# Conv pieces of a deformable layer in other slots of a hand-written schedule

## The chip, the core and the metric

The kernel runs on one core of one Trainium2 chip. The metric is the device time of one execution in microseconds, here the median of several runs. Engine names: PE is TensorE, DVE is VectorE, ACT is ScalarE, POOL is GpSimd, SP is SyncE, whose queue issues most of the DMAs.

## What is computed

A net of four layers over x[8, 384, 32, 32] in fp32: a state-space layer, a deformable layer, a second state-space layer with an MLP, and a displacement layer. Each adds its result to its input after a group norm. The change is in the deformable layer only:

```python
def deform_block(x, ow, ob, dw, pw, pb, K):
    offsets = conv2d(x, ow, ob, K // 2)              # 2*K*K maps: dy, dx of every tap
    out = deform_depthwise(x, offsets, dw, K, K // 2)  # bilinear samples, weighted, summed over taps
    return conv2d(out, pw, pb, 0)                    # 1x1

c3, c5, c7 = jnp.split(x, 3, axis=1)                 # 128 channels each
out = jnp.concatenate([deform_block(c3, ..., 3), deform_block(c5, ..., 5), deform_block(c7, ..., 7)], axis=1)
return out * se_weight(out, fc1_w, fc2_w)
```

with x the group norm of the layer's input (32 groups, so mean and variance over 12 channels and all 1024 pixels).

## The kernel before

The layer is `deform_fast`. It handles the 8 samples one after the other, and of each sample three blocks: 3x3, 5x5, 7x7. The taps of a block are gathered in fours ("quads"; the last one has a single tap), and each quad is done in two halves. One half of one quad is a **unit**: 6 units in the 3x3 block, 14 in the 5x5 block, 26 in the 7x7 block, 46 in a sample, 368 in all.

A unit needs four steps. SP loads the sampling positions (`positions`, L1417). ACT turns them into bilinear "hat" functions in x and y (`unit_hats`, L1433 to L1451; the x hats are made once for both halves, with the first). DVE weighs the transposed input (`fxk`, L1469) and multiplies x and y hats into products (`fsm`, L1486, five buffers). PE multiplies the two and adds into five PSUM banks (`wacc`, L1516).

All of this stands in a hand-written order. Time is cut into **slots**, one for each unit. In slot u the program emits the position loads of unit u+4, the products of PE for unit u, the DVE work of unit u+1 and the hats of unit u+2; the loop is at the end of `deform_fast`. Everything else is put into a slot by `put(slot, place, fn, ...)` in `block_steps`, where place says the engine (`pe`, `dve`, `act`) and whether it comes ahead of the slot's unit work (`pe0`, `dve0`, `act0`) or behind it (`pe1`, `dve1`, `act1`). For PE, DVE and ACT this order is kept as it is written (`manual_schedule`). The engines are not tied to one another but for their data, so a slot has no fixed length.

The slots concerned, by name:

- `first[b, g]` is the slot of the first unit of block g (0, 1, 2 for 3x3, 5x5, 7x7) of sample b; `s0` is that of the block at hand. The 3x3 and 5x5 blocks together have 20 slots, the 7x7 block 26.
- For g = 0 the base t is `s0 - 26`, which is the start of the 7x7 block of the sample in front. From there on, in that block: the load of the new sample (`load`, L1096), group-norm statistics (`stats`, L1102, DVE), group means by a matmul (`mean`, L140), deviations (`dev`), their squares on ACT (`square`, L167), a second matmul (`mean2`, L150), variance, 1/std on ACT with two table loads (`rstd`, L181 and L182), then the normalisation of each third of the channels (`norm`, L1126, DVE), and last the 3x3 conv in one piece of 36 matmuls (`conv`, L1195, PE) and the step that takes its result (`offsets`, L1206 to L1217: add, write to DRAM, maxima and minima).
- For g = 1 the 5x5 conv has 50 matmuls in six pieces, one a slot, also in the 7x7 block in front.
- For g = 2 the 7x7 conv is done as a fast convolution (`fir`, L1157) in three parts with 21, 28 and 28 matmuls of up to 512 columns. `fir_sum` (L1143, DVE) makes the sums of even and odd columns that part 0 reads. After each part its result is taken from PSUM: `fir_take` on ACT for part 0 (L1166), on DVE for parts 1 and 2 (L1171). `fir_end` (L1178 to L1182) adds the grid, finds maxima and minima, and writes the positions.
- All three convs use one PSUM bank (`ps_off`, tag "conv", one buffer), so each conv or part starts after the one ahead of it has been read.

At the start of each block, `sums_act` closes the old accumulation with five matmuls of zeros (L1254), ACT and DVE add its banks up (L1256 to L1262), and `begin` opens the new one with five more (L1397). Around there the transposed input is made too: `rows_pe` (L1223) and `cells_pe` (L1243) on PE, copied out by ACT (L1230, L1248). `point` (L1268) is the 1x1 conv, `squeeze` (L1281 to L1283) the sums and maxima of the squeeze gate.

Of the kernel before, what the change touches and what calls it, by code (L numbers as in the profile page):

```python
# [17 lines left out]
G = C // P  # L18
# [73 lines left out]
class Net:  # L92
# [984 lines left out]
    def block_steps(self, b, g, first, put, weights, src, dst):  # L1077
        nc, K = self.nc, KS[g]
        K2, pad = K * K, K // 2
# [246 lines left out]
        if g == 0:  # L1326
            t = s0 - 2 * len(QUADS[KS[-1]])
            put(t + 1, "act0", load)
            for i in range(G):
                put(t + 2 + i, "dve1", stats, i)  # L1330
            put(t + 6, "pe0", mean)
            put(t + 6, "dve1", dev)
            put(t + 7, "act1", square)
            put(t + 8, "pe0", mean2)
            put(t + 8, "dve1", var)
            put(t + 9, "act1", rstd)
            for i in range(G):
                put(t + 10 + i, "dve1", norm, i)
            put(t + 13, "pe1", conv, 0, 0, K2)
            put(t + 14, "dve0", offsets, 0)  # L1340
        elif g == 1:
            t = first[b, 0] - 12
            for i in range(6):
                put(t + i, "pe1", conv, 0, K2 * i // 6, K2 * (i + 1) // 6)
            put(t + 6, "dve0", offsets, 0)
        else:
            t = first[b, 0]
            put(t - 1, "dve1", fir_sum)
            k = 0
            for part, pieces in enumerate((4, 5, 5)):  # L1350
                nw = K * len(FIR[part])
                for i in range(pieces):
                    where = "pe0" if t + k in (first[b, 0], first[b, 1]) else "pe1"
                    put(t + k, where, fir, part, nw * i // pieces, nw * (i + 1) // pieces)
                    k += 1
                put(t + k, "dve0" if part else "act0", fir_take, part)
            put(t + k, "dve0", fir_end)
# [490 lines left out]
```

## Time and profile before

| | us |
|---|---|
| median of 3 runs | 9464.09 |
| lowest, highest | 9463.35, 9469.98 |
| profiled execution | 9470.15 |
| its span, first to last instruction | 9468.3 |
| mean granted TensorE clock | 0.947 |
| PE busy in the span | 8498.2 |
| DVE busy | 8092.7 |
| ACT busy | 6476.0 |

The profile is one execution taken by the hardware profiler. A timeline row has the start in us, the duration, the engine, the line of the kernel, the operation, output and input by the program's names, the shape and the number of instructions merged into the row; in brackets the idle time of the engine ahead of it, and what ended that. One fp32 matmul leaves two records. A row of the windows table has the length of the window and, for each engine, the busy time in it with the number of instructions, then the granted TensorE clock, the busy share of the DMA engines, and GB/s.

The deformable layer lies between about 3031 and 5862 us. The zeroing at L1397, which opens a block, begins at 3117.78 for the first 3x3 block and at 3457.07, 3802.93, 4150.08, 4495.93 for the next samples' 3x3 blocks; the 7x7 blocks of the first three samples open at 3273.64, 3618.10 and 3963.95. Other rows of use:

| row | number |
|---|---|
| 7x7 conv matmuls (L1157), records | 1232 |
| 3x3 and 5x5 conv matmuls (L1195), records | 1376 |
| products on PE (L1516), records | 10624 |
| PE waiting for DVE's products ahead of L1516, in all | 240.5 us, 278 times |
| DVE waiting for PE ahead of the products of L1486, in all | 315.6 us, 320 times |

### The profile page before, as it was taken

Reading aid. Unit: us, or ns where it says so; the run is one execution under the profiler, and the core shown is the slowest. Engines: PE = TensorE matmul, PEld = TensorE weight load, DVE = VectorE, ACT = ScalarE, POOL = GpSimd, SP = SyncE. Lnnn points to the kernel's source line nnn. Section 1 sums busy time; section 2 is a strip of 40 time slices with the busy share of each in tenths; the row PEclk is TensorE's granted clock in tenths of the full one; section 3 lists DMA queues with packets and bytes.
Section 4 is the critical chain, followed back from the end, with each engine's and each line's share of the span. In section 5 each row is a group of like instructions: output and inputs, shape, how many; then the busy total and the mean of one; then the engine's idle time right before and its main releaser. Section 6 shows DMA issues by size and latency. Waiting matters only on the chain. (4 is left out here: it accounts for less than half of the span.)

```text
span 9468.3 us, 87246 instructions
## 1 busy us (share of the span) xinstructions
PE 8498.2 (90%) x27916; PEld 4527.1 (48%) x27916; DVE 8092.7 (85%) x8857; ACT 6476.0 (68%) x10147; POOL 5825.0 (62%) x3825
## 2 busy tenths in 40 slices
PE   7888888889887999999999997699999999999987
PEld 3333333333333677777777776244343443434333
DVE  7989999999997678778778877899999999999973
ACT  6666666666664678778778777667777777777750
POOL 7989989898897000000000000899999999999974
PEclk8999999999998999999999998799999999999998
DMA  2111211121121333333333333233232433323436
GB/s 94 66 56 46 85 56 49 52 83 56 50 79 40 80 77 89 92 80 88 89 83 87 90 80 87 93 99 96 90 95 88 126 107 96 92 91 90 123 99 127
DMA packets 566064, 791.97 MB, mean 84 GB/s; under 512 B 244243, under 2 KB 397235, under 8 KB 542041
## 3 DMA queue, kind: packets, MB, share of 16 engines
q1 hardware_dynamic: 503492, 775.85, 28.2%
q10 hardware_dynamic: 62100, 10.44, 0.7%
q8 instruction: 223, 3.65, 0.2%
q14 instruction: 249, 2.03, 0.1%
HBM read 716.49 MB, written 69.66 MB: 83 GB/s over the span
## 5 line engine op out<-in xcount | busy, mean ns | idle before, releaser
L443 POOL TENSOR_TENSOR db<-du,bc 128x1024 f32<-128x1024 f32 x1536 | 3607.0, 2354 | 356.3 <-DVE hs L453 184.7
L453 DVE TENSOR_TENSOR_SCAN da<-da,db 128x1024 f32<-128x1024 f32 x1248 | 2857.4, 2290 | 220.5 <-ACT da L438 170.0
L484 PE MATMUL y<-hs,ident 128*128 128x512 f32 x5184 | 2602.9, 639 | 382.2 <-DVE hs L467 229.8
L438 ACT ACTIVATE da<-dt,na 128x512 f32<-128x512 f32 x3072 | 2119.4, 691 | 917.0 <-DVE hs L467 653.8
L411 POOL TENSOR_TENSOR dt<-dt,sp_e 128x512 f32<-128x512 f32 x192 | 243.9, 1270 | 2929.1 <-DVE sp_e L403 2929.1
L484 PEld LDWEIGHTS y<-hs,ident 128*128 128x128 f32 x5184 | 1020.4, 203 | 1860.6 <-issue 1115.9
L1516 PE MATMUL wacc<-fsm,fxk 128*128 128x221 f32 (+34 forms) x10624 | 1667.7, 316 | 91.5 <-DVE fsm L1486 88.8
L1516 PEld LDWEIGHTS wacc<-fsm,fxk 128*128 128x128 f32 x10624 | 1580.6, 196 | 228.4 <-DVE fsm L1486 151.7
L467 DVE TENSOR_TENSOR hs<-da,bc 128x1024 f32<-128x1024 f32 x1248 | 1528.5, 1225 | 91.7 <-DVE da L453 2.3
L1486 DVE TENSOR_TENSOR fsm<-fhy,fhx 128x170 f32<-128x170 f32 (+42 forms) x3216 | 1171.5, 431 | 342.5 <-PE wacc L1516 315.6
L1446 ACT ACTIVATE fhy<-fpyx,cell 128x416 f32<-128x416 f32 (+9 forms) x1280 | 645.6, 576 | 386.8 <-DVE fsm L1486 386.8
L1469 DVE TENSOR_TENSOR fxk<-fxt,fwk 128x1024 f32<-128x1024 f32 (+1 forms) x688 | 788.2, 1182 | 10.8 <-ACT fxt L1248 10.8
L464 POOL TENSOR_TENSOR hs<-hs,bc 128x1024 f32<-128x1024 f32 x288 | 678.3, 2355 | 41.7 <-ACT st L459 41.6
L453 DVE TENSOR_TENSOR_SCAN hs<-da,db 128x1024 f32<-128x1024 f32 x288 | 656.8, 2280 | 49.0 <-POOL db L431 36.1
L471 POOL TENSOR_TENSOR hs<-hs 128x512 f32<-128x512 f32 x480 | 608.9, 1268 | 4.0 <-DVE hs L467 3.5
L567 PE MATMUL ps_m<-hid,wm 128*128 128x512 f32 x1152 | 536.8, 611 | 30.2 <-ACT hid L560 25.3
L545 PE MATMUL ps_h<-t,wm 128*128 128x512 f32 x1152 | 535.9, 603 | 16.5 <-DVE x L574 16.3
L1451 ACT ACTIVATE fhy<-fhy,cols 128x1344 f32<-128x1344 f32 (+10 forms) x368 | 530.8, 1442 | 12.0
L459 ACT COPY st<-da 128x2 f32<-128x2 f32 x624 | 97.8, 157 | 504.3 <-DVE hs L467 503.0
L1157 PE MATMUL ps_off<-fxn,fow 128*98 128x465 f32 (+10 forms) x896 | 386.6, 579 | 0.0
L1433 ACT ACTIVATE fhx<-fpyx,cell 128x544 f32<-128x544 f32 (+8 forms) x640 | 379.9, 666 | 0.0
L567 PEld LDWEIGHTS ps_m<-hid,wm 128*128 128x128 f32 x1152 | 221.6, 195 | 330.8 <-issue 262.4
(203 smaller groups left out, 9865.4 us busy)
## 6 DMA issues: line engine op xcount, KB each, us to landing
bc<-bcd SPq DMA_DIRECT2D x256, 1024.0 KB
fpyx<-fposd SPq DMA_DIRECT2D x640, 256.0 KB
wm<-in_w SPq DMA_DIRECT2D x96, 768.0 KB
x<-x SPq DMA_DIRECT2D x71, 768.0 KB
winr<-in_win SPq DMA_DIRECT2D x192, 192.0 KB
x<-in_x SPq DMA_DIRECT2D x40, 768.0 KB
fpyx<-fposd SPq DMA_DIRECT2D x24, 1024.0 KB
wm<-in_wout SPq DMA_DIRECT2D x48, 384.0 KB
```

The lines of the kernel that those rows point to most:

```text
L438: nc.scalar.activation(da[:, i, :], s["dt", j], AF.Exp, scale=na[:, j, n : n + 1])
L443: nc.gpsimd.tensor_tensor(db, du, s["bc"][m][:, 0], ALU.mult)
L453: nc.vector.tensor_tensor_scan(h1, da1, db1, 0.0, ALU.mult, ALU.add)
L464: nc.gpsimd.tensor_tensor(s["hs", m], s["hs", m], c, ALU.mult)
L467: nc.vector.tensor_tensor(hs, s["da", m], c, ALU.mult)
L471: nc.gpsimd.tensor_tensor(hs[:, 0, :], hs[:, 0, :], hs[:, 1, :], ALU.add)
L484: nc.tensor.matmul(s["y"], self.ident, s["hs", m][:, i, :], start=first and i == 0, stop=k == NU - 1 and i == n - 1,)
L567: nc.tensor.matmul(ps, s["w2"][:, f, o * P : (o + 1) * P], s["hid", q][:, f, :], start=(f == 0), stop=(f == 3))
L1446: nc.scalar.activation(hy[:, at : at + (yb - ya) * W], pyx[:, 0, ya * W : yb * W], AF.Abs, bias=bias)
L1469: nc.vector.tensor_tensor(t[:, :n], x, wk[:, j : j + 1, :].to_broadcast([P, n, P]), ALU.mult)
L1486: nc.vector.tensor_tensor(self.sub(sm, at, [(r * w, n), (w, r), (1, w)]), self.sub(hy, hy_at[by] + xa, [(r * W, n), (W, r), (1, w)]), self ...
L1516: nc.tensor.matmul(a[:, ya - 4 * o : yb - 4 * o, xa:xb], k, self.sub(sm, sm_at[by], [(w, yb - ya), (1, w)]), start=False, stop=False,)
```

## The change

Only the slots change, for all three convs and for the group norm ahead of them. Counted in the 7x7 block in front (slots 0 to 25) and in the sample's own 3x3 and 5x5 blocks ("front" slots 0 to 19):

| step | before | after |
|---|---|---|
| `stats` 0, 1, 2 | 7x7 slots 2, 3, 4 | 2, 2, 3 |
| `mean`, `dev` | 6 | 5 |
| `square` | 7 | 6 |
| `mean2`, `var` | 8 | 7 |
| `rstd` | 9 | 8 |
| `norm` 0, 1, 2 | 10, 11, 12 | 9, 9, 9 |
| 3x3 conv, `offsets` | 13, 14 | 10, 11 |
| 5x5 conv, pieces | 6 pieces in 14 to 19 | 7 pieces in 11 to 17 |
| 5x5 `offsets` | 20 | 18 |
| `fir_sum` | 25 | 16 |
| 7x7 conv, part 0 | 4 pieces in front slots 0 to 3 | 7 pieces in 7x7 slots 18 to 24 |
| its `fir_take` | front slot 4 | 7x7 slot 25 |
| part 1 | 5 pieces in front slots 4 to 8 | 8 pieces in 7x7 slot 25 and front slots 0 to 6 |
| its `fir_take` | front slot 9 | front slot 7 |
| part 2 | 5 pieces in front slots 9 to 13 | 7 pieces in front slots 7 to 13 |
| its `fir_take`, `fir_end` | front slot 14 | front slot 14 |

The first sample has no block in front of it; its steps have the same slots ahead of its unit 0, with no unit work beside them.

```diff
         if g == 0:
             t = s0 - 2 * len(QUADS[KS[-1]])
             put(t + 1, "act0", load)
-            for i in range(G):
-                put(t + 2 + i, "dve1", stats, i)
-            put(t + 6, "pe0", mean)
-            put(t + 6, "dve1", dev)
-            put(t + 7, "act1", square)
-            put(t + 8, "pe0", mean2)
-            put(t + 8, "dve1", var)
-            put(t + 9, "act1", rstd)
-            for i in range(G):
-                put(t + 10 + i, "dve1", norm, i)
-            put(t + 13, "pe1", conv, 0, 0, K2)
-            put(t + 14, "dve0", offsets, 0)
+            for i, k in enumerate((2, 2, 3)):
+                put(t + k, "dve1", stats, i)
+            put(t + 5, "pe0", mean)
+            put(t + 5, "dve1", dev)
+            put(t + 6, "act1", square)
+            put(t + 7, "pe0", mean2)
+            put(t + 7, "dve1", var)
+            put(t + 8, "act1", rstd)
+            for i, k in enumerate((9, 9, 9)):
+                put(t + k, "dve1", norm, i)
+            put(t + 10, "pe1", conv, 0, 0, K2)
+            put(t + 11, "dve0", offsets, 0)
         elif g == 1:
-            t = first[b, 0] - 12
-            for i in range(6):
-                put(t + i, "pe1", conv, 0, K2 * i // 6, K2 * (i + 1) // 6)
-            put(t + 6, "dve0", offsets, 0)
+            t = first[b, 0] - 15
+            for i in range(7):
+                put(t + i, "pe1", conv, 0, K2 * i // 7, K2 * (i + 1) // 7)
+            put(t + 7, "dve0", offsets, 0)
         else:
-            t = first[b, 0]
-            put(t - 1, "dve1", fir_sum)
+            t = first[b, 0] - 8
+            put(t - 2, "dve1", fir_sum)
             k = 0
-            for part, pieces in enumerate((4, 5, 5)):
+            for part, pieces in enumerate((7, 8, 7)):
                 nw = K * len(FIR[part])
                 for i in range(pieces):
                     where = "pe0" if t + k in (first[b, 0], first[b, 1]) else "pe1"
                     put(t + k, where, fir, part, nw * i // pieces, nw * (i + 1) // pieces)
```

## The prediction

> **What bounds the kernel now.** I read the windows by stage first, because the whole-kernel page says only that TensorE (PE) is busy for 90% of the span and VectorE (DVE) for 85%. The change touches the middle layer alone (about 3031 to 5862 us). In the trace that layer repeats every 345.86 us: the weighted convolution begins its matmuls for the 3x3 block at 3359.83, 3705.69, 4052.84 and so on. Here are the windows of one period: tail of the 5x5 block, 7x7 block in three parts, then the next sample's 3x3 block and start of its 5x5 block.
>
> ```profile
> core 0: us, PE busy (x) PEld busy (x) DVE busy (x) ACT busy (x) POOL busy (x), PEclk, DMA share, GB/s
> 3577.00:3618.00 41.00, 34.30 (x234) 31.82 (x232) 37.18 (x78) 29.20 (x44) 0.00 (x0) 0.92 0.33 91
> 3618.00:3705.70 87.70, 78.37 (x455) 72.06 (x456) 83.83 (x170) 82.11 (x114) 0.00 (x0) 0.94 0.38 93
> 3705.70:3761.80 56.10, 56.10 (x366) 41.97 (x365) 42.19 (x90) 44.49 (x58) 0.00 (x0) 1.00 0.34 77
> 3761.80:3797.00 35.20, 33.17 (x218) 31.79 (x218) 35.06 (x73) 24.71 (x38) 0.00 (x0) 1.00 0.23 66
> 3797.00:3853.00 56.00, 54.42 (x284) 35.18 (x282) 32.79 (x68) 37.56 (x62) 0.00 (x0) 1.00 0.34 95
> 3853.00:3877.00 24.00, 22.30 (x96) 13.24 (x95) 15.99 (x34) 21.99 (x34) 0.00 (x0) 1.00 0.27 66
> 3877.00:3924.00 47.00, 47.00 (x227) 30.58 (x226) 31.69 (x60) 31.17 (x45) 0.00 (x0) 1.00 0.38 101
> ```
>
> Two regimes alternate. Wherever a slot holds conv pieces (3705 to 3762, 3877 to 3924) PE is busy for 100% and DVE for 67 to 75%: PE-bound. Where it holds none (3577 to 3705, 3762 to 3797) DVE is busy for 91 to almost 100% and PE waits for it. ScalarE (ACT) is full at block starts. PE's timeline gives the sizes, with the idle time ahead of a row and its releaser in brackets:
>
> ```profile
> 3693.25 12.51 PE L1516 MATMUL wacc<-fsm,fxk 128*128 128x121 f32 x64 [1.57 <-DVE fsm L1486]
> 3705.69 4.01 PE L1195 MATMUL ps_off<-fxn,fow 128*32 128x256 f32 x72
> 3709.62 5.00 PE L1516 MATMUL wacc<-fsm,fxk 128*128 128x120 f32 x32
> 3714.55 3.57 PE L1195 MATMUL ps_off<-fxn,fow 128*64 128x512 f32 x16
> ...
> 3767.19 5.29 PE L1516 MATMUL wacc<-fsm,fxk 128*128 128x156 f32 x32 [0.66 <-DVE fsm L1486]
> 3772.66 4.89 PE L1516 MATMUL wacc<-fsm,fxk 128*128 128x60 f32 x32 [0.18 <-DVE fsm L1486]
> ...
> 3798.95 4.14 PE L1157 MATMUL ps_off<-fxs,fow 128*98 128x512 f32 x10
> 3802.93 1.24 PE L1397 MATMUL wacc<-zero 128*128 128x512 bf16 x5
> 3804.01 1.73 PE L1516 MATMUL wacc<-fsm,fxk 128*128 128x160 f32 x8
> 3806.34 1.14 PE L1243 MATMUL ps_t<-ident,frep 128*128 128x128 f32 x8 [0.60 <-ACT fxt L1248]
> ```
>
> A 7x7 unit (32 records at L1516) takes PE 4.8 to 5.5 us, mean 5.09 over the PE-bound ones. A 7x7 matmul of the fast convolution, two records, costs about 0.82 us (all 14 pieces, 77 matmuls, add up to 63.2 us from start to start). The third fence is DVE in the conv-free part, one slot: a weighting of 2.35, products of 3.7, and an extra:
>
> ```profile
> 3682.96 2.35 DVE L1469 TENSOR_TENSOR fxk<-fxt,fwk 128x1024 f32<-128x1024 f32 x2
> 3685.23 3.74 DVE L1486 TENSOR_TENSOR fsm<-fhy,fhx 128x260 f32<-128x260 f32 x12
> 3688.88 0.81 DVE L1126 TENSOR_SCALAR fxn<-fxn,gn_rstd,gn_nb 128x1024 f32<-128x1024 f32 x1
> ...
> 3761.87 0.75 DVE L1206 SCALAR_TENSOR_TENSOR fpos<-ps_off,fobk,fgrid 128x512 f32<-128x512 f32 x1 [4.49 <-PE ps_off L1195]
> ```
>
> So a 7x7 slot costs DVE 5.95 us and PE 5.09: PE has almost 0.9 us of room per slot there, and with three fast-conv matmuls (2.5 us) in it, it would cost PE 7.6 us.
>
> **What the Trainium skill says.** "Perfetto Trace Analysis", Optimization Strategy: where a kernel has several regimes with different most-contended engines, interleaving them can help. The trace agrees that there are two regimes, and spreading the conv pieces is such an interleaving. "PSUM — Partial Sum Buffer", Engine vs sequencer instructions: matmuls start and complete in program order, and the ScalarE and VectorE queues are strict FIFO. The trace agrees: the pieces run in the slots where the code puts them. "TensorE: Matmul & The Clock Gate", What's actually happening: a PE that is idle for a window of about 3.4 us drops to half clock. The trace has the same direction (0.92 to 0.94 in the parts with gaps, 1.00 in the dense ones), though its means of a window can't show the two states.
>
> **The change part by part.** No instruction is added or taken away; the same 36, 50 and 77 conv matmuls change slots. So the sum is over PE's idle time. "Front slots" are the 20 slots of a sample's 3x3 and 5x5 blocks, "7x7 slots" the 26 after them.
>
> (a) 7x7 slots 10 to 13. Before, the 3x3 conv comes after unit 13, at 3705.69, and ends at 3709.62. After, it follows unit 10. DVE still has the same work up to there (statistics earlier, same total): the products of unit 10 end at 3682.96, then come the three normalisations at once, 3 x 0.75, so 3685.2. The group-norm chain costs a little: moved a slot up, the square (0.15 us) now stands behind the hats of an even unit, x and y (3655.08 to 3663.05), where it stood behind y alone. So PE reaches the second mean at about 3659.3 and waits for it until 3663.1; the mean's 2.17 us end at 3665.4. Unit 7 is then some 3.5 us late, PE makes up 0.9 per slot, and DVE isn't held, since the five fsm buffers are still freed in time (unit 7's first group at 3666.7, wanted at 3668.3). PE then ends unit 10 at about 3685.7. The conv's 3.93 us and units 11 to 13 at 5.09 follow without a gap: 3704.9 instead of 3709.62. Gain 4.7 us; bounds 2.5 (the chain holds DVE) and 5.2 (it costs nothing).
>
> (b) 7x7 slots 20 to 25 get fast-conv pieces of three matmuls, so they turn PE-bound: PE's waits there (0.66, 0.18, 0.26 and 0.94) go. Gain 2.0 us; bounds 1.0 and 2.5. In slots 11 to 25 PE has 7.6 to 8.2 us a slot, DVE 5.95 plus at most 2.4 for the offsets, ACT 5.75: neither comes late. The sum for the 5x5 offsets' max and min still sits between conv and next conv in the one conv bank, but behind it PE has a unit of 5.1 us to do; DVE needs 2.4. The read of the first part by ACT (0.69) at 7x7 slot 25 likewise has unit 25 beside it. There ACT waits for PE's slot 24, and the next sample's hats and cell copies (1.05, 2.7) queue behind it; PE's slot 25 (7.6 us) covers those 4.4 us.
>
> (c) Front slots 0 to 13 keep 53 of the 77 matmuls, three or four to a slot instead of five or six. A slot falls from 8.6 us to about 7.2; DVE has 5 us of work on average there, with the squeeze (2.5 us) in one slot of each block, and it runs one unit ahead (unit 4's first product is ready at 3824.8, PE wants it at 3834.43), so it stays hidden. But at slots 0 and 6 PE waits for a chain on ACT from L1254 on (block sums, hats, cell copies), and the piece there is shorter: four matmuls instead of five, 3.3 instead of 3.98 and 3.4 instead of 4.25 us. The wait in front of L1243 grows by as much. Loss 0.65 + 0.85 = 1.5 us; bounds 1.0 and 3.0.
>
> (d) The work moved in SP's queue: the writes of the 3x3 offsets pass eight position loads, those of the 5x5 offsets four. The loads behind them are wanted two slots later, so nothing. The sum of even and odd columns (0.7 us of DVE) moves nine slots up into a PE-bound slot: nothing.
>
> Per sample 4.7 + 2.0 - 1.5 = 5.2 us. Seven of the eight 7x7 blocks carry convs (nothing follows the last sample): 36 us.
>
> (e) The start. Before, the 5x5 conv ends at 3100.15 and unit 0 starts at 3118.86; PE idles between. After, 12 fast-conv matmuls stand in front of the transposes: PE waits for DVE's reads of the 5x5 offsets (3102.5), works to 3112.7, then transposes (1.0), three matmuls, cells, three, cells, three, ACT's read, three, cells, four, the zeroing (1.1). I add these up to 3133.4 with the hats (5.0 us on ACT) behind the transposes, so unit 0 is 14.5 us late, but 28 matmuls are done instead of 5: 23 x 0.82 = 18.9. Net gain 4.4, less the 0.85 of slot 6: 3.5 us; bounds -5 (the matmuls run at the 0.95 us each that the first cold piece shows, and ACT's chain adds up) and +8.
>
> Sum: 36.4 + 3.5 = 40 us off. The durations come from the profiled execution, 9470.15 us with a span of 9468.3, 0.06% over the median of 9464.09; the difference applies to either: 9424 against the median.
>
> **Rivals.** (1) The gain stays, but small: the group-norm chain, squeezed to two slots a step, holds DVE in the conv-free part. For it: ACT is busy for 94% there, and the chain has two table loads of 1.28 us on ACT. Against: the five fsm buffers as counted in (a), and a DVE that never waited for ACT there longer than 0.95 us. If the whole of (a) is lost, 7 x 0.5 + 3.5 = 7 us stay: 9457. (2) Slower, by the granted clock: PE with fewer gaps draws a lower clock in the dense slots. For it: PEclk is 0.75 to 0.89 in the 100 us windows just behind this layer (5800 to 6200), so the chip does withhold clock. Against: in this layer the densest windows have 1.00. PE-bound work is about 250 us of each period, 2000 us in all; at 0.96 that costs 83 us less the 40: 9507. It decides from 2% of clock on.
>
> **How the numbers follow.** Likeliest with 0.68: 9424, its own range 9408 to 9444 from the bounds above. Rival 1 with 0.18: 9457. Rival 2 with 0.14: 9507. About 0.2% (19 us) is what a measurement of this kernel can tell from no change. Nearly all of the first case is faster by more: 0.67; no change 0.18; slower 0.15. The range must take in rival 1 as well: 9404 to 9474.
>
> **What would show it.** Right: a period of 340.6 instead of 345.86 us; the 3x3 conv some 68 us after its 7x7 block's zeroing (87.6 before); no PE idle behind it up to the block's end; the wait at front slots 0 and 6 longer by 0.65 and 0.85; unit 0 near 3133. Wrong: DVE idle in 7x7 slots 3 to 9, or waiting for ACT there; PE idle in front slots 2 to 13; PEclk under 0.98 in dense windows; a period over 344.

## The result, and the profile after

| | before | after |
|---|---|---|
| median, us (16 runs each, side by side) | 9466.08 | 9449.67 |
| ratio, 95% interval | | 0.9982 (0.9974 to 0.999) |
| profiled execution's span, us | 9468.3 | 9445.1 |
| zeroing of the first 3x3 block (L1397) to that of the last sample's, us | 2418.3 | 2404.0 |
| mean period of the six samples from the second on, us | 346.5 | 344.5 |

It is faster by 16.4 us where 40 were forecast: the direction is right, the size is 0.4 of it. The trace shows that the part with conv pieces became what it should. These are windows of the changed kernel over one 7x7 block: from its zeroing to the 3x3 conv, and from there in two parts nearly to its end:

```profile
core 0: us, PE busy (x) PEld busy (x) DVE busy (x) ACT busy (x) POOL busy (x), PEclk, DMA share, GB/s
3613.00:3684.40 71.40, 62.72 (x357) 56.54 (x357) 65.06 (x131) 64.44 (x91) 0.00 (x0) 0.93 0.39 96
3684.40:3750.50 66.10, 66.10 (x429) 51.13 (x429) 54.79 (x114) 51.22 (x66) 0.00 (x0) 1.00 0.31 71
3750.50:3806.00 55.50, 55.50 (x298) 44.64 (x297) 43.46 (x90) 37.77 (x54) 0.00 (x0) 1.00 0.29 74
```

PE is busy without a gap from 3684.4 to 3806, where it waited for DVE in 7x7 slots 20 to 25 before. But the first row is too long and DVE is idle in it: the 3x3 conv starts 71.3 us after this block's zeroing, 73 after that of later samples, where I had worked out some 68. PE's timeline of the sample after, in the stretch of the group norm, shows the place:

```profile
3987.93 2.07 PE L140 MATMUL gn_ps<-gn_mv,gmat 128*128 128x2 f32 x18
3989.86 9.79 PE L1516 MATMUL wacc<-fsm,fxk 128*128 128x169 f32 x64
4002.78 4.00 PE L150 MATMUL gn_ps<-gn_dm,gmat 128*128 128x1 f32 x18 [3.13 <-ACT gn_dm L167]
4006.63 22.26 PE L1516 MATMUL wacc<-fsm,fxk 128*128 128x180 f32 x128
4028.82 4.00 PE L1195 MATMUL ps_off<-fxn,fow 128*32 128x256 f32 x72
```

PE idles 3.13 us ahead of the second mean (L150). That was foreseen, and so was its reason, the square behind a pair of hats on ACT:

```profile
3998.82 2.18 ACT L1446 ACTIVATE fhy<-fpyx,cell 128x352 f32<-128x352 f32 x4
4001.03 1.63 ACT L1451 ACTIVATE fhy<-fhy,cols 128x1600 f32<-128x1600 f32 x1
4002.57 0.15 ACT L167 ACTIVATE gn_dm<-gn_ps 128x3 f32<-128x3 f32 x1
```

Not foreseen: the mean takes 4.00 us (in six of the seven samples; 3.07 in the other), twice the 2.07 of its twin at L140. And DVE is held behind it, which the sum had excluded. DVE's timeline in slot 7, after and then before (the slot of the mean was slot 8 there; this is one of the three samples in which DVE waits 1.9 us, in the other four it is 0.35):

```profile
4005.48 0.75 DVE L1486 TENSOR_TENSOR fsm<-fhy,fhx 128x110 f32<-128x110 f32 x2
4009.16 1.11 DVE L1486 TENSOR_TENSOR fsm<-fhy,fhx 128x187 f32<-128x187 f32 x2 [2.93 <-PE wacc L1516]
4011.86 1.11 DVE L1486 TENSOR_TENSOR fsm<-fhy,fhx 128x187 f32<-128x187 f32 x2 [1.59 <-PE wacc L1516]
4013.49 1.01 DVE L1486 TENSOR_TENSOR fsm<-fhy,fhx 128x165 f32<-128x165 f32 x2 [0.51 <-PE wacc L1516]
```

```profile
4019.11 1.68 DVE L1486 TENSOR_TENSOR fsm<-fhy,fhx 128x260 f32<-128x260 f32 x6
4022.10 1.04 DVE L1486 TENSOR_TENSOR fsm<-fhy,fhx 128x442 f32<-128x442 f32 x3 [1.31 <-PE wacc L1516]
4023.75 0.95 DVE L1486 TENSOR_TENSOR fsm<-fhy,fhx 128x390 f32<-128x390 f32 x3 [0.60 <-PE wacc L1516]
```

After, the three waits add up to 5.03 us in this sample and to 33.6 over the seven blocks (3.7, 3.8, 5.0, 5.2, 5.3, 5.3, 5.3), where the kernel before has 7.1 in all. DVE is what this stretch is bound by, so each of these microseconds counts. Windows of 2 us on PE alone (length, busy time, records, then granted clock, DMA share, GB/s) say why PE is that slow:

```profile
3998.00:4000.00 2.00, 1.64 (x12) 1.00 0.25 49
4000.00:4002.00 2.00, 0.00 (x0) 1.00 0.00 0
4002.00:4004.00 2.00, 1.23 (x6) 0.50 0.01 4
4004.00:4006.00 2.00, 2.00 (x11) 0.50 0.00 0
4006.00:4008.00 2.00, 2.00 (x9) 0.50 0.98 238
4008.00:4010.00 2.00, 2.00 (x8) 0.50 0.94 217
4010.00:4012.00 2.00, 2.00 (x8) 0.50 0.35 70
4012.00:4014.00 2.00, 2.00 (x15) 0.94 0.00 0
```

The granted clock is cut to half during the gap and stays there for some 10 us, through the mean and most of unit 7. In five of the seven samples the stretch at half clock lasts 10.24 us, in the first two 6.83. The Trainium skill describes this kind of mechanism in "TensorE: Matmul & The Clock Gate", What's actually happening: half rate after an idle window of about 3.4 us. The prediction named it and then didn't price it: its own numbers make PE wait 3.8 us (3659.3 to 3663.1), and I used full-clock durations for everything behind that. An idle gap alone doesn't explain the trace, though: the gap is 3.13 us, less than the window named there, and in the kernel before, with gaps of 0.77 to 1.03 us ahead of this mean, the clock is halved behind it too. The last section comes back to this.

### The profile page after: what moved, and what is told of

It is laid out like the page before. It is cut to its first block, busy times and chain, and to the rows that moved or that the text cites. A ratio compares the mean times of both kernels' runs of the same rounds, so it can differ in the third digit from the quotient of the medians.

```text
span 9445.1 us, 87192 instructions
## 1 busy us (share of the span) xinstructions
PE 8474.7 (90%) x27891; PEld 4510.8 (48%) x27916; DVE 8099.1 (86%) x8857; ACT 6482.0 (69%) x10147; POOL 5829.1 (62%) x3825
## 3 DMA queue, kind: packets, MB, share of 16 engines
q14 instruction: 248, 2.03, 0.1%
```

## The experiments

All times below are medians beside runs of the kernel before on the same chip (9467.8 us for the first four, 9470.2 for the last two); the ratio is to those.

**The second mean behind unit 7.** Nothing else moves but the variance, which needs the mean's result.

```diff
-            put(t + 7, "pe0", mean2)
-            put(t + 7, "dve1", var)
+            put(t + 7, "pe1", mean2)
+            put(t + 8, "dve0", var)
```

> The changed kernel with one step placed elsewhere: the second group mean stands behind unit 7's matmuls instead of ahead of them (the variance one place later on DVE, so that it follows). In the changed kernel PE idles 3.1 to 3.3 us ahead of that mean, then runs it and unit 7 slowly, and DVE waits 3.7 to 5.3 us for PE in slot 7 of every 7x7 block, 33.6 us over the seven. Theory A (that stall is what ate the gain of slots 10 to 13): DVE's waits there go to under 1 us, the 3x3 conv starts about 67.5 us after the block's zeroing instead of 71.3 to 73, the period falls from 344.5 to about 340, the time to 9416 to 9425. Theory B (the chain through ACT and DVE is the limit in any place, and the stall only comes back at the normalisation or the hats): the time stays within 8 us of the changed kernel's 9450.

Measured: 9410.54 us, ratio 0.994 (0.9926 to 0.9953). Theory A holds, and the gain is even larger than expected. The waits of DVE are gone in all seven blocks, and the 3x3 conv starts 66.6 to 67.1 us after the zeroing. DVE's products in slot 7 are one row without a bracket:

```profile
3996.78 3.70 DVE L1486 TENSOR_TENSOR fsm<-fhy,fhx 128x110 f32<-128x110 f32 x8
```

PE's timeline of the same stretch:

```profile
3991.41 4.99 PE L1516 MATMUL wacc<-fsm,fxk 128*128 128x180 f32 x32 [0.69 <-DVE fsm L1486]
3996.24 2.10 PE L150 MATMUL gn_ps<-gn_dm,gmat 128*128 128x1 f32 x18
3998.20 16.43 PE L1516 MATMUL wacc<-fsm,fxk 128*128 128x110 f32 x96
4014.56 4.00 PE L1195 MATMUL ps_off<-fxn,fow 128*32 128x256 f32 x72
```

By the time PE has done unit 7, the square is ready: no bracket ahead of L150, and 2.10 us for it. The period is 338.34 us in four of the samples.

**The gap filled with zeros.** The mean stays ahead of unit 7, as in the change, but PE isn't idle while it waits for ACT.

```diff
+        def fill():
+            if b:
+                acc = self.state[b - 1, G - 1]["acc"]
+                for i in range(15):
+                    nc.tensor.matmul(acc[:, i % NB, :], self.zero[:, :P], self.zero, start=False, stop=False)
...
+            put(t + 7, "pe0", fill)
             put(t + 7, "pe0", mean2)
```

> The changed kernel with 15 matmuls of zeros (about 0.21 us each, 3.2 us in all, added to the open sums, so nothing changes in the result) ahead of the second group mean, in the place where PE idles. PE still can't start the mean earlier, it only isn't idle. Theory A1 (it is the clock: idle PE falls to a slower clock, so the mean takes 4.0 us instead of 2.1 and unit 7's first groups 2.6 instead of 1.27): the mean takes about 2.1 us, DVE's waits in slot 7 fall from 3.7 to 5.3 us to under 1, the time falls to 9417 to 9427. Theory A2 (it is the wait alone): DVE's waits stay above 3 us and the time within 8 us of 9450, or above it by the zeros.

Measured: 9428.37 us, ratio 0.9956 (0.9943 to 0.997), so 21 us below the changed kernel for work that computes nothing. PE's timeline (L1119 are the zeros; the products stand at L1523 on PE and at L1493 on DVE here):

```profile
4000.34 3.40 PE L1119 MATMUL wacc<-zero 128*128 128x512 bf16 x15
4003.61 2.17 PE L150 MATMUL gn_ps<-gn_dm,gmat 128*128 128x1 f32 x18
4005.64 21.19 PE L1523 MATMUL wacc<-fsm,fxk 128*128 128x180 f32 x128
```

The mean takes 2.17 us in all seven samples, and DVE's waits in slot 7 fall from 33.6 to 11.6 us in all. So Theory A1 holds for the larger part: keeping PE at work made 22 of the 33.6 us go. The time is 1.4 us above the expected range, and waits under 1 us were reached in two of the seven samples only, the first two. These two tell the rest apart, since there the clock stays full behind the mean; in the other five it falls later, for 3.41 us. DVE's waits in the second and in the third sample, and PE's windows of the third:

```profile
3668.64 1.11 DVE L1493 TENSOR_TENSOR fsm<-fhy,fhx 128x187 f32<-128x187 f32 x2 [0.26 <-PE wacc L1523]
3669.99 1.01 DVE L1493 TENSOR_TENSOR fsm<-fhy,fhx 128x165 f32<-128x165 f32 x2 [0.24 <-PE wacc L1523]
...
4009.60 1.11 DVE L1493 TENSOR_TENSOR fsm<-fhy,fhx 128x187 f32<-128x187 f32 x2 [1.47 <-PE wacc L1523]
4011.42 1.01 DVE L1493 TENSOR_TENSOR fsm<-fhy,fhx 128x165 f32<-128x165 f32 x2 [0.71 <-PE wacc L1523]
```

```profile
4006.00:4008.00 2.00, 2.00 (x12) 0.74 0.43 127
4008.00:4010.00 2.00, 2.00 (x8) 0.50 1.10 258
4010.00:4012.00 2.00, 2.00 (x14) 0.90 0.69 139
```

At full clock the late mean thus costs DVE 0.5 us a sample. With 3.41 us at half clock behind it, it is 2.0 to 2.2 us, and with the 6.83 to 10.24 us of the changed kernel 3.7 to 5.3.

**The group norm alone in the new slots**, convs and offsets in the old ones:

```diff
-            for i in range(G):
-                put(t + 2 + i, "dve1", stats, i)
-            put(t + 6, "pe0", mean)
...
+            for i, k in enumerate((2, 2, 3)):
+                put(t + k, "dve1", stats, i)
+            put(t + 5, "pe0", mean)
...
             put(t + 13, "pe1", conv, 0, 0, K2)
             put(t + 14, "dve0", offsets, 0)
```

> The kernel before with the group-norm steps alone in the new slots; all conv pieces and their result steps stay in the old ones. Theory A: the stall in slot 7 appears here too, DVE waits 3.7 to 5.3 us there instead of 0 to 1.9, and nothing is gained in return: 7 x 3 to 4 us slower, 9485 to 9495. Theory B, or that the conv pieces cause the stall: within 8 us of the kernel before, 9466.

Measured: 9489.38 us, ratio 1.0023 (1.0015 to 1.0032), 21.6 slower. DVE waits 29.0 us for PE behind the mean over the seven blocks, 21.9 more than in the kernel before, close to the time lost. The stall comes with the group norm and not with the conv pieces:

```profile
4017.31 4.00 PE L150 MATMUL gn_ps<-gn_dm,gmat 128*128 128x1 f32 x18 [3.10 <-ACT gn_dm L167]
```

**The 7x7 conv in its old pieces and slots**, the rest of the change kept:

```diff
-            t = first[b, 0] - 8
-            put(t - 2, "dve1", fir_sum)
+            t = first[b, 0]
+            put(t - 1, "dve1", fir_sum)
             k = 0
-            for part, pieces in enumerate((7, 8, 7)):
+            for part, pieces in enumerate((4, 5, 5)):
```

> The changed kernel with the 7x7 conv back in its old 14 pieces and slots; group norm, 3x3 and 5x5 conv in the new slots. Then 7x7 slots 18 to 25 hold no conv: DVE-bound, so PE loses what it gained in slots 20 to 25 (2.0 us) and another 1.8 in slots 18 and 19, and the start gains nothing. Theory A: the gain of slots 10 to 13 is eaten by the stall in slot 7, so this is slower than the kernel before by 5 to 20 us: 9471 to 9486. Rival (the spread of the 3x3 and 5x5 conv alone makes the measured 16 us): about 9450.

Measured: 9473.68 us, ratio 1.0007 (0.9998 to 1.0015): inside the range of theory A, and well above the rival's 9450. The interval doesn't tell it from the kernel before. So without the move of the 7x7 conv the changed kernel is 24 us slower, and the group norm, 3x3 and 5x5 conv together bring no gain that can be told: DVE waits 28.9 us behind the mean here.

**Longer pieces at the block starts**, on top of the mean behind unit 7. It tests step (c), and whether a better version lies there.

```diff
+                cuts = (0, 3, 8, 10, 13, 16, 19, 22, 28) if part == 1 else [nw * i // pieces for i in range(pieces + 1)]
                 for i in range(pieces):
                     where = "pe0" if t + k in (first[b, 0], first[b, 1]) else "pe1"
-                    put(t + k, where, fir, part, nw * i // pieces, nw * (i + 1) // pieces)
+                    put(t + k, where, fir, part, cuts[i], cuts[i + 1])
```

> On top of the kernel with the second mean behind unit 7 (9410.5): the same 28 matmuls of part 1, but cut so that the pieces at front slots 0 and 6 have 5 and 6 matmuls instead of 4 and 4, and those in slots 1 to 5 fewer (14 instead of 17; the slot ahead of slot 0 keeps 3). Theory (step (c) of the prediction: from the closing zeros L1254 on, slots 0, 1, 6 and 7 last as long as ACT's chain, so a matmul there is free and a matmul elsewhere costs 0.83 us): the waits ahead of L1243 fall from 1.3 and 2.0 us to about 0.5 and 0.3, the period by 2.5 us, eight blocks 20 us: 9388 to 9396. Rival (a longer piece delays the opening zeros and everything behind them): within 6 us of 9410.

Measured: 9388.83 us, ratio 0.9917 (0.9904 to 0.9931), in the range. The waits of PE at the two starts, first in the changed kernel, then here:

```profile
3472.00 1.14 PE L1243 MATMUL ps_t<-ident,frep 128*128 128x128 f32 x8 [1.32 <-ACT fxt L1248]
...
3475.80 1.98 PE L1268 MATMUL ps_pw<-fdsb,pwt 128*128 128x512 f32 x4 [0.98 <-ACT fxt L1248]
...
3520.21 1.60 PE L1243 MATMUL ps_t<-ident,frep 128*128 128x128 f32 x8 [1.97 <-ACT fxt L1248]
```

```profile
3800.99 1.14 PE L1243 MATMUL ps_t<-ident,frep 128*128 128x128 f32 x8 [0.50 <-ACT fxt L1248]
...
3804.78 1.98 PE L1268 MATMUL ps_pw<-fdsb,pwt 128*128 128x512 f32 x4 [0.97 <-ACT fxt L1248]
...
3846.76 1.14 PE L1243 MATMUL ps_t<-ident,frep 128*128 128x128 f32 x8 [0.34 <-ACT fxt L1248]
```

**Two pieces ahead of the unit in front slots 1 and 7**, on top of that:

```diff
-                    where = "pe0" if t + k in (first[b, 0], first[b, 1]) else "pe1"
+                    where = "pe0" if t + k in (first[b, 0], first[b, 0] + 1, first[b, 1], first[b, 1] + 1) else "pe1"
...
-                put(t + k, "dve0" if part else "act0", fir_take, part)
+                if part == 1:
+                    put(t + k - 1, "dve1", fir_take, part)
+                else:
+                    put(t + k, "dve0" if part else "act0", fir_take, part)
```

> On top of the run with long pieces at the block starts: the pieces of front slots 1 and 7 stand ahead of the slot's unit, between the cell transposes and it, instead of behind the 1x1 conv (DVE's reading of part 1 one place earlier, in slot 6, so that part 2 can begin). PE then has work while it waits 0.8 to 1.0 us for ACT ahead of L1268. Theory: these two waits go, 1.8 us a sample, 14 us: 9374 to 9384. Rival (the wait only moves behind, or the later 1x1 conv makes ACT and the squeeze late): within 6 us of the run with long pieces.

Measured: 9376.86 us, ratio 0.9901 (0.9886 to 0.9916). The waits ahead of L1268 in these two slots are gone. Of their 1.8 us a sample, 0.90 comes back two slots after the first, where a small matmul of the squeeze gate (L1288) waits for ACT and didn't before:

```profile
3800.71 1.88 PE L1268 MATMUL ps_pw<-fdsb,pwt 128*128 128x512 f32 x4
...
3810.47 0.31 PE L1288 MATMUL ps_f<-am,f 128*24 128x2 f32 x6 [0.90 <-ACT fxt L1230]
```

This is the fastest version of the study, 1.0% below the kernel before and 0.8% below the changed one by the ratios.

## Why the prediction was right in parts

**Step (a) failed**, in this sentence: "Unit 7 is then some 3.5 us late, PE makes up 0.9 per slot, and DVE isn't held, since the five fsm buffers are still freed in time (unit 7's first group at 3666.7, wanted at 3668.3)." It took everything behind PE's wait at full clock. The slack was 1.6 us, and it rested on 2.17 us for the mean and 1.27 for a group of unit 7. At half clock the mean took 4.00 and unit 7's first two groups of eight records 2.3 and 2.7. So DVE waited 33.6 us over seven blocks, as much as step (a) was to bring (7 x 4.7 = 32.9). With the stall taken away and all else kept, the time is 9410.5, which is 57 us below the kernel before beside it and 17 more than forecast. Some 5 of these 17 are waits of the kernel before that the prediction's sample didn't show (1.9 us in three samples for its 0.35) and that vanish as well; the rest isn't accounted for. The changed kernel, too, kept more than the 7 us that rival 1 left over with the whole of (a) lost. Rival 1 was the right rival with half of the cause: it had ACT's late result, not the clock, and "against" it stood the same buffer count. The lower bound of (a), 2.5 us, had no number behind it; with a clock of a half it would have been about zero.

The profile of before held the warning. Its L150 rows have a gap of 0.77 to 1.03 us, and half clock follows in all seven samples, for 3.41 us in four and 6.83 us in three. In these three, every second sample, the mean takes 2.95 to 3.15 us and DVE waits 1.9, as in the rows shown above. The period before alternates with them, between 345.85 and 347.16 us. I took one sample's rows and its shorter period for all, though two of the three times that the prediction names, 3705.69 and 4052.84, are 347.15 apart.

**Step (b) is right**: PE's idle time from the 3x3 conv to the block's end is 0.06 us in every sample, for 2.03 before. **Step (c) is right in kind** and a little small: PE's waits at slots 0 and 6 grew by 0.72 and 1.08 us (from 0.60 and 0.89), 1.8 where 1.5 stood. The run with longer pieces confirms it: matmuls moved back under ACT's chain were free, 21.7 us by the medians, 24 when each run is set against the kernel before beside it, for 20 expected. **Step (d) is right**: SP's position loads wait 20.6 us in all for the writes of offsets, 20.5 before, and the one wait of an engine for positions that the trace lists is 0.3 us. **Step (e)** is right: the zeroing ahead of unit 0 is 12.9 us later (3130.70 for 3117.78) against 14.5, and the first front part is 17.2 us shorter (138.68 for 155.86), a net gain of 4.3 where 3.5 stood. **Rival 2 is excluded**: the dense windows keep a clock of 1.00. The clock did decide, but in the opposite way: through too little work of PE, not through load.

The sum over the profiled layer, in measured parts: eight front parts, 15.8 to 17.2 us shorter each, seven 7x7 blocks 13.7 to 15.3 us longer, the start 12.9 us longer, in all 17.9 us less.

## What to carry to other kernels

When TensorE waits ahead of a row of narrow matmuls, take the wait and these matmuls together as one pause: here about 1 us of wait with the mean behind it brought 3.4 to 6.8 us at half clock, and 3.1 us of wait with it 6.8 to 10.2. Price what runs behind such a pause at half clock as well, and then ask again whether the other engine's buffers last. A small matmul whose input comes late belongs behind the large ones that are ready: ahead of them it left PE idle for 3.1 us, behind them it didn't wait. And where another engine's chain sets the length of a slot, put the movable matmuls there and take them out of the slots that TensorE sets.

## What was not expected of the hardware

The clock was also cut where PE had no gap. With the mean behind unit 7, PE is busy throughout, yet in two of that run's seven samples half clock follows the mean's 18 one-column records. In all eight traces the stretches at half clock in this layer start on a grid of 3.41 us, one for each trace, and last whole steps of it. These are PE's windows of that run cut to the grid, in a sample with the mean at 3996.24 and in one with it at 4673.81. First all of PE's work, then the products alone (length, busy time, records, then granted clock, DMA share, GB/s):

```profile
3996.05:3999.46 3.41, 3.41 (x32) 1.00 0.63 139
3999.46:4002.87 3.41, 3.41 (x12) 0.50 0.80 168
...
4671.88:4675.29 3.41, 3.41 (x30) 1.00 0.14 24
4675.29:4678.70 3.41, 3.41 (x25) 1.00 1.01 228
```

```profile
3996.05:3999.46 3.41, 1.61 (x14) 1.00 0.63 139
...
4671.88:4675.29 3.41, 2.09 (x16) 1.00 0.14 24
4675.29:4678.70 3.41, 2.93 (x19) 1.00 1.01 228
```

The first mean lies within one step and leaves 1.61 us of it to products; the next step is at half clock. The second lies across two steps, and the clock stays. The whole layer agrees (3040 to 5840 us, all eight traces, steps at full clock). Where PE did something other than the two means (L140, L150) for 60% of a step or more, half clock followed in none of 5767 steps; where it did so for less than 35%, in all 143; in between, in 78 of 214. With the means counted as work, half clock followed 25 steps that were busy for 60% or more, 18 of them for 90% or more, and each of the 25 held part of a mean. So in these traces matmuls of one or two columns count as if PE were idle, or nearly. In the run with zeros the same step to half clock follows the mean in five samples, about 1 us behind its end. No run varied the width of these matmuls alone, so whether it is the width or something else in them stays open.
